# A four-layer graph network on one core: adding DMAs for the last mixture of experts, and GATv2 products and weight loads moved

## The chip, the cores and the metric

The kernel runs on one core of a Trainium2 chip, as one launch. The metric is the device time of that core in microseconds (us), the median of the runs. Engines are TensorE (PE in the profile, PEld for its weight loads), VectorE (DVE), ScalarE (ACT), GpSimd (POOL) and SyncE (SP). SP, ACT and POOL also issue DMAs; POOL issues the indirect ones, which gather or scatter rows by an index.

## What is computed

The input is a graph of 1250 nodes with 512 features, 20,000 edges and a loop at each node. Four layers follow one another. Each adds three things to the features `x`: a graph convolution and an attention over all nodes, both of the normed features, and then a feed-forward part (FFN).

- Layer 0: GATv2, itself three layers (per edge `leaky_relu(xl[src] + xr[dst] + ef)`, a logit, a softmax over each target's edges, a weighted sum of `xl[src]`); linear attention; eight experts with Sinkhorn routing.
- Layer 1: GAT, two layers; full attention over all nodes; eight experts of which two are taken.
- Layer 2: EGConv; linear attention; ten experts of which two are taken.
- Layer 3: GCN; linear attention; 32 experts with a capacity, of which two are taken.

The last FFN of the reference, which the change rewrites, is this (two experts a node, K = 2, and C = 98 rows an expert):

```python
C = int(np.ceil(CAPACITY_FACTOR * BTK / N))
probs = jax.nn.softmax(x_flat @ Wg, axis=-1)
vals, idx = jax.lax.top_k(probs, K)
...
keep = pos < C
dest = jnp.where(keep, a * C + pos, N * C)
buf = jnp.zeros((N * C, D), x.dtype).at[dest].set(x_flat[token], mode='drop')
h = jax.nn.relu(jnp.einsum('ncd,ndh->nch', buf, W1) + b1[:, None, :])
o = (jnp.einsum('nch,nhd->ncd', h, W2) + b2[:, None, :]).reshape(N * C, D)
gathered = o[jnp.minimum(dest, N * C - 1)]
y_flat = jax.ops.segment_sum(gathered * w[:, None], token, num_segments=BT)
y_flat = jnp.where(contrib[:, None] <= 1e-12, x_flat, y_flat)
```

## The kernel before

Nodes lie on the partitions in ten tiles of 128 (`NT`); the last one has 98 nodes. Most products are fp32 on PE, 128 rows by 512 columns in four steps over the features. The framework orders each engine's instructions and puts in the waits; where the code says `manual_schedule(engines={Pool})`, POOL's instructions keep the order in which they are written. Each engine runs its own queue in order, its DMA issues among them. SBUF and PSUM buffers rotate in pools, so that a load into a buffer waits for the last reader of what it held.

*GATv2* (`gat_layer`, one call for each of three layers). Edges come in groups of four tiles of 128, four groups for a block of 103 targets. For a group, POOL gathers the source rows `xl` from a table in DRAM (`load`, through `gather`, L231), SP loads an index row `nb` and edge fields into `oh` (`fields`, L1257 and L1259), ACT makes a one-hot matrix of them (`onehot`, L1273), PE spreads the target rows over the edges with it (`right`, L1286, L1287, and L1289, which adds `xl` on PE in every second of the first 20 steps), DVE forms the logits (L1299, L1302), and PE sums up by target (L1353). `load` runs three groups ahead of the edge steps and `fields` two. When a block of targets is done, a short list of steps (`finish`) norms it, transposes it (`across`, L1409) and, as soon as a whole tile of 128 nodes is there, makes the next layer's two tables for it (`gat_tables`): four products with `wl` and a store into `tl` (L1184), and four with `wr` and a store into `tr` (L1189), L1166 being the product. They pass through the queue `late` and take one PSUM bank, named `tab`. At the end of a layer a loop empties the queues; tiles 7, 8 and 9 come only there or shortly before. Gathers of the next layer read any row of `tl`, and so wait for its last store. From step 6 on, `prepare` loads the next layer's weights and vectors and works out its small vectors, a piece every third step.

*Layer 0's FFN* (`layer0_ffn`). Eight experts, each product's rows stored into `obuf` from ACT. Then 20 gathers on POOL bring back two rows for each node, DVE adds them by the gates (`add_scaled`, L1811), norms a tile, and PE transposes it (L160). Layer 1's attention (`global_attention`) loads four weights of 1 MB through `weight` (L141), and SP issues these as soon as a buffer is free. In the same stretch a counting of edges by pairs (L711) runs on PE between other steps, fed by loads on SP.

*Layer 2's FFN to layer 3* (`layer3_attn`). The experts' rows are stored into `routed_out` (L2367); `tail_steps` gives a function `need(t)`, which brings tile t of `xn` up through gathers (L231), adds (L2887), a norm and an affine step (L2896, L2897), a norm for the next layer and a transpose (L2386). SP loads four weights of 1 MB at the start (L141): the GCN's and three of the linear attention, of which ACT scales the last by 0.125 (L762).

*Layer 3's FFN* (`layer3_ffn`). 64 weight matrices of 1 MB stream in on SP (L3051), eleven ahead. Routing is worked out for all nodes at once on DVE. POOL scatters the normed rows into `routed_in` (20 DMAs, L239), at the row expert × 98 + place. Beside that, PE and DVE add the gated second biases, and the rows themselves for a node without an expert, into `x` (L3153, L185, L1811). For each expert ACT loads 98 rows `xe` (L3160), PE transposes them (L3164), DVE copies (L136), PE makes two products (L179 with ACT's relu, L3169; then L3173), the result is copied (L134 on ACT or L136 on DVE in turn) and stored into `routed_out` from ACT. After all 32, 20 gathers bring each node's two rows, `add_scaled` adds them by their gates, and SP stores each tile of `x` to the output.

Of the kernel before, what the change touches and what calls it, by code (L numbers as in the profile page):

```python
# [23 lines left out]
N = 1250  # L24
# [33 lines left out]
class Net:  # L58
# [79 lines left out]
    def weight(self, src, k, n):  # L138

        w = self.wp.tile([128, k, n], F32, tag="w", name="w")  # L140
        self.nc.sync.dma_start(w, src.rearrange("(k p) n -> p k n", p=128))  # L141
        return w
# [591 lines left out]
    def linear_attention_steps(self, xn, xT, w_qkv, w_out, b_out, qscale, finish, added=None,  # L734
                               need=None):
# [14 lines left out]
        with self.tc.tile_pool(name="la", bufs=1) as p, \  # L750
                self.tc.tile_pool(name="latmp", bufs=2) as tmp:
            wk = self.weight(w_qkv[:, D:2 * D], 4, D)
            wv = self.weight(w_qkv[:, 2 * D:3 * D], 4, D)
# [4 lines left out]
            for half in range(2):  # L758
                if half:
                    wq = self.weight(w_qkv[:, 0:D], 4, D)  # L760
                    if qscale != 1.0:
                        nc.scalar.mul(wq, wq, qscale)  # L762
# [446 lines left out]
    def gat_layer(self, L, p, xtab, otab, big):  # L1209
# [27 lines left out]
        step = [0]  # L1237

# [16 lines left out]
        def fields(g):  # L1255
            nb = p.tile([128, GE * 128], BF16, tag="nb", name="nb", bufs=4)
            nc.sync.dma_start(nb, self.nbt[g])  # L1257
            s = p.tile([128, GE * 128], F32R, tag="oh", name="oh", bufs=3)
# [102 lines left out]
        def finish(b):  # L1361
# [44 lines left out]
            def across():  # L1406
# [10 lines left out]
                for t in whole:  # L1417
                    for f in self.gat_tables(nxt, p, t, lambda c, t=t: X[t][:, c, :],
                                             lambda: self.bank("tab", [128, D])):
                        late.append((step[0] + 1, f))  # L1420
# [37 lines left out]
        fields(1)  # L1458
        onehot(0)
        prepared = prepare()  # L1460
        for i in range(FT + 3):
# [9 lines left out]
            if j == 2 and g + 2 < FG:  # L1471
                fields(g + 2)
            if i >= 6 and i % 3 == 0:
# [20 lines left out]
        bias_cur(NB - 1)  # L1494
        while edge or todo or late:
# [6 lines left out]
            for _ in range(2):  # L1502
                if late:
                    late.popleft()[1]()
        return nxt
# [24 lines left out]
    def layer0_ffn_to_layer1_attn(self):  # L1530
# [11 lines left out]
        with self.tc.tile_pool(name="l1a", bufs=1) as p:  # L1542
            xnT = p.tile([128, 4, NP], F32, name="xnT")
            with self.tc.tile_pool(name="l1b", bufs=1) as pb:
                xn = pb.tile([128, NT, D], F32, name="xn")
                with self.weights(), self.psum(3, 2, 3) if fast else self.psum():
                    count_pool()
                    self.counting = self.count_blocks(range(CB), True) if fast else iter(())
                    self.layer0_ffn(xn, xnT)
# [7 lines left out]
                    self.global_attention(xn, xnT, steps)  # L1557
# [91 lines left out]
    def layer0_ffn(self, xn, xnT):  # L1649
# [6 lines left out]
        with self.tc.tile_pool(name="l0f", bufs=1) as p, \  # L1656
# [126 lines left out]
            for t in range(NT):  # L1783
                for j in range(2):
                    g = tmp.tile([128, D], F32, tag="g", name="g", bufs=6)
                    self.gather(g, obuf[:, :], getI[:, t, j:j + 1])
                    self.add_scaled(t, g, G[:, t, j:j + 1])
                self.ready(t)
                self.norm_tile(t, xn[:, t, :])
                self.transpose_tile(xnT[:, :, t * 128:(t + 1) * 128], xn[:, t, :])  # L1790
                self.count(1)
            g1.close()

# [12 lines left out]

# [1451 lines left out]
```

## Time and profile before

| | |
|---|---|
| runs, us | 4461.85, 4464.39, 4471.24; median 4464.39 |
| profiled execution, us | 4489.82, span 4487.9 |
| mean granted clock of TensorE | 0.937 |
| last GATv2 product of a layer and the next layer's first (first boundary) | 750.93 and 765.70 |
| the same, second boundary | 1184.7 and 1189.32 |
| layer 0's FFN: first gather of `obuf`, PE idle before its next step | 1815.83, 16.24 |
| layer 2's FFN: first gather of `routed_out`, PE idle before its next step | 3736.03, 27.85 |
| layer 3's FFN: last scatter landed, first L179 product | 4200.62, 4204.76 |
| layer 3's FFN: last product ends, span ends | 4443.46, 4487.9 |

All times are microseconds from the start of the profiled span, or durations. In the page, a group is a line of the kernel, engine, operation, output and inputs, with its busy time and mean duration, and behind the last bar the time for which its engine stood idle before it and what ended that. In a table of windows each row gives a stretch, the busy time of each engine in it with the number of instructions, TensorE's granted clock, the share of the DMA engines' time and the rate. In a timeline a row gives start, duration, engine, line, operation and names, and in brackets the idle time before. In the chain of waits a row gives start, duration, and the work or wait that held up the end.

### The profile page before, as it was taken

How to read it: one execution, taken by the hardware profiler on the slowest of the kernel's cores; microseconds unless marked ns; L12 is line 12 of the kernel's file. 1: busy time of each engine (PE TensorE's matmuls, PEld its weight loads, DVE VectorE, ACT ScalarE, POOL GpSimd, SP SyncE). 2: the span in 40 equal slices, each digit the busy share in tenths (PEclk: the TensorE clock that was granted, in tenths of full speed). 3: DMA queues.
4: the chain of work that ended last, by engine and by line, in shares of the span. 5: the costliest groups of instructions: out<-in, count | busy, mean ns of one | idle time of the engine just before them, and what ended most of it. 6: DMA issues, size and time to landing. Idle time of an engine off the chain costs nothing. (4 is left out here: it accounts for less than half of the span.)

```text
span 4487.9 us, 49486 instructions
## 1 busy us (share of the span) xinstructions
PE 3922.2 (87%) x15466; PEld 2415.7 (54%) x15466; DVE 2689.5 (60%) x6338; ACT 1622.8 (36%) x2976; POOL 1351.0 (30%) x1308
## 2 busy tenths in 40 slices
PE   5987998899788867799999999997979896898796
PEld 3434554455354434444788877563546562455474
DVE  5357895888398865523896767314584225687301
ACT  2222442344133375110464446223451232554121
POOL 2017773776466501102000000103131013675102
PEclk9988999999899988899999999999989998997798
DMA  6437664666466423402421110383002653666695
GB/s 220 159 84 211 198 199 150 198 197 193 141 179 189 145 74 108 119 17 64 146 70 42 46 35 29 143 298 128 12 27 83 233 189 119 182 200 199 225 339 181
DMA packets 283001, 647.58 MB, mean 144 GB/s; under 512 B 61673, under 2 KB 108905, under 8 KB 267322
## 3 DMA queue, kind: packets, MB, share of 16 engines
q1 hardware_dynamic: 169290, 357.13, 24.1%
q0 software_dynamic: 73088, 234.75, 18.3%
q10 hardware_dynamic: 40352, 52.44, 3.4%
q8 instruction: 127, 2.08, 0.2%
q14 instruction: 144, 1.18, 0.1%
HBM read 528.87 MB, written 120.65 MB: 145 GB/s over the span
## 5 line engine op out<-in xcount | busy, mean ns | idle before, releaser
L231 POOL DMA_INDIRECT xl<-xl,srcI x564 | 616.8, 1094 | 290.2 <-issue 137.8
L1353 PE MATMUL more<-xl,wT 128*128 128x512 f32 x1128 | 579.7, 601 | 14.5 <-ACT wT L1343 14.0
L1286 PE MATMUL mm<-hl,oh 121*128 121x512 f32 x564 | 419.1, 743 | 73.8 <-DVE s L1299 37.8
L1302 DVE SCALAR_TENSOR_TENSOR junk<-s,att 128x512 f32<-128x512 f32 x534 | 417.9, 783 | 6.8
L1299 DVE TENSOR_TENSOR s<-xl,mm 128x512 f32<-128x512 f32 x534 | 357.8, 679 | 104.0 <-PE mm L1287 48.4
L2129 PE MATMUL more<-hh,e 128*128 128x259 f32 x1600 | 383.7, 385 | 11.7 <-ACT o L2072 8.6
L2129 PEld LDWEIGHTS more<-hh,e 128*128 128x128 f32 x1600 | 295.1, 191 | 75.8 <-issue 17.8
L171 PE MATMUL mm<-w,xnT 128*128 128x512 f32 x640 | 307.8, 620 | 16.6 <-ACT xnT L2388 12.1
L231 POOL DMA_INDIRECT hs<-gcn_h,srcI x188 | 214.6, 1142 | 93.6 <-issue 30.8
L1353 PEld LDWEIGHTS more<-xl,wT 128*128 128x128 f32 x1128 | 196.1, 192 | 74.8 <-issue 27.9
L1287 PE MATMUL mm<-hl,oh 121*128 121x512 f32 x564 | 236.4, 419 | 0.0
L1286 PEld LDWEIGHTS mm<-hl,oh 121*128 121x128 f32 x564 | 111.0, 197 | 215.5 <-issue 117.1
L231 POOL DMA_INDIRECT g<-routed_out,getI x60 | 67.6, 1126 | 488.5 <-DMA routed_out<-o 416.4
L2049 ACT ACTIVATE e<-r,hh 128x512 f32<-128x512 f32 (+1 forms) x240 | 154.2, 646 | 130.7 <-PE more L2129 119.5
L171 PEld LDWEIGHTS mm<-w,xnT 128*128 128x128 f32 x640 | 123.4, 198 | 144.0 <-issue 124.6
L3011 PE MATMUL more<-hl,oh 128*128 128x512 f32 x376 | 161.5, 534 | 30.9 <-DVE oh L2975 10.9
L1273 ACT ACTIVATE oh<-nb 112x512 fp32r<-112x512 bf16 x141 | 88.7, 630 | 273.6 <-DMA nb<-nbt 162.3
L2052 ACT ACTIVATE e<-r,a 128x512 f32<-128x512 f32 (+1 forms) x240 | 152.3, 646 | 71.1 <-DVE e L2054 57.8
L711 PE MATMUL more<-ohs,ohb 128*128 128x512 bf16 x564 | 137.5, 383 | 42.8 <-ACT ohs L695 18.0
L2054 DVE TENSOR_TENSOR e<-e,e 128x512 f32<-128x512 f32 (+1 forms) x240 | 141.5, 596 | 51.2 <-ACT e L2049 44.8
L1287 PEld LDWEIGHTS mm<-hl,oh 121*128 121x128 f32 x564 | 112.4, 199 | 110.1 <-issue 108.4
L1166 PE MATMUL tab<-w,xT 128*128 128x512 f32 x320 | 163.5, 605 | 9.0 <-ACT xT L1415 6.1
(631 smaller groups left out, 7787.8 us busy)
## 6 DMA issues: line engine op xcount, KB each, us to landing
w<-L_ffn_Wp SPq DMA_DIRECT2D x64, 1024.0 KB
w<-L_ffn_table SPq DMA_DIRECT2D x56, 1025.0 KB
neg<-ntab SPq DMA_DIRECT2D x80, 320.0 KB
nb<-nbt SPq DMA_DIRECT2D x141, 128.0 KB
hl<-xr SPq DMA_DIRECT2D x36, 448.0 KB
xr<-tro SPq DMA_DIRECT2D x30, 512.0 KB
xe<-routed_in SPq DMA_DIRECT2D x56, 256.0 KB
routed_out<-o ACTq DMA_DIRECT2D x56, 256.0 KB
```

Source lines behind the costliest of these rows:

```text
L171: self.nc.tensor.matmul(p, lhsT=xT[:, c, t * 128:(t + 1) * 128], rhs=w[:, c, n0:n0 + n], start=c == 0, stop=c == k - 1)
L231: self.nc.gpsimd.indirect_dma_start(out=out, out_offset=None, in_=table, in_offset=bass.IndirectOffsetOnAxis(ap=idx, axis=0), bounds_check ...
L1166: nc.tensor.matmul(d[name], lhsT=xT(c), rhs=L[name][:, c, :], start=c == 0, stop=c == 3)
L1286: nc.tensor.matmul(m, lhsT=s, rhs=hl[:K, 0, :], start=True, stop=False)
L1287: nc.tensor.matmul(m, lhsT=s, rhs=hl[:K, 1, :], start=False, stop=not on_pe(i))
L1299: nc.vector.tensor_tensor(o, d["xl"][:, j, :D], s, op=ALU.add)
L1302: nc.vector.scalar_tensor_tensor(junk, s, 0.0, L["att"], op0=ALU.max, op1=ALU.mult, accum_out=d["lg"][:, j:j + 1])
L1353: nc.tensor.matmul(B[b]["y"], lhsT=d["wT"][:, j, :], rhs=d["xl"][:, j, :D], start=k == 0 and j == 0, stop=last and j == GE - 1)
L2049: nc.scalar.activation(e1[:, :n], R[q, k, 0][:, :n], AF.Exp, bias=HH[q][:, s, 256:257])
L2052: nc.scalar.activation(e2[:, :n], R[q, k, 1][:, :n], AF.Exp, bias=heads[q][0][:, s, 0:1])
L2129: nc.tensor.matmul(ys[j], lhsT=e[:, j * 128:(j + 1) * 128], rhs=HH[q][:, s, :], start=s == 0, stop=s == NT - 1)
L3011: nc.tensor.matmul(y, lhsT=oh, rhs=hl[:, i], start=i + j == 0 and not (self.fast and k), stop=last and i + j == GE)
```

## The change

Five things change; the rest stays.

- *Layer 3's FFN.* The normed rows are two words wider (`xn` is 514 wide): the first of the two holds the node's number, which `iota` writes. They are scattered into a table of their own, `rin3`, which `clear_places` has filled beforehand with zeros and with row numbers beyond the nodes (1280 and up). A second table, `gtab`, holds for each node its first expert's number and its two gates. After the biases each tile of `x` is stored to the output on ACT. The node numbers of all places are loaded at once, in four DMAs on ACT (`tok`), ahead of the loads of `xe`. For each expert POOL gathers the gates of its rows from `gtab` (`fetch`), five experts ahead; DVE picks the one that belongs to this expert (`d`, three operations on 98 × 1), multiplies the result by it on its way out of PSUM, and POOL adds the 98 rows into the output by an indirect DMA with `compute_op=ALU.add`. The 32 stores, 20 gathers, 20 adds and ten output stores at the end are gone. The output has 1408 rows rather than 1250: rows 1280 and up take the unused places, and the host keeps the first 1250.
- *GATv2 products by target.* Of tiles 7, 8 and 9 the four `wr` products and the store into `tr` are held back and issued by the next layer, after its first `fields`, `load` and `onehot` and before its first step. In the ending loop the table products take `mm` banks rather than the `tab` bank.
- *GATv2 fields.* `fields` runs three groups ahead rather than two, with a fifth buffer for `nb` and a fourth for `oh`; `prepare` begins at step 15 rather than 6.
- *Layer 0's FFN to layer 1.* Of the attention's weights only `wk` is loaded ahead of the gathers; `wv` is loaded behind a POOL `memset` that stands after the last gather in POOL's fixed order. `clear_places` issues 34 stores on SP at the start of layer 1's attention.
- *Layer 2's FFN to layer 3.* The three weights of the linear attention are loaded behind three POOL `memset`s that come after `need(0)`; the GCN's weight stays where it was.

The core of the diff:

```diff
-    def weight(self, src, k, n):
+    def weight(self, src, k, n, behind=False):
 
         w = self.wp.tile([128, k, n], F32, tag="w", name="w")
+        if behind:
+            self.nc.gpsimd.memset(w[:1, 0, :1], 0.0)
...
-            nb = p.tile([128, GE * 128], BF16, tag="nb", name="nb", bufs=4)
+            nb = p.tile([128, GE * 128], BF16, tag="nb", name="nb", bufs=5)
...
-            s = p.tile([128, GE * 128], F32R, tag="oh", name="oh", bufs=3)
+            s = p.tile([128, GE * 128], F32R, tag="oh", name="oh", bufs=4)
...
-                    for f in self.gat_tables(nxt, p, t, lambda c, t=t: X[t][:, c, :],
-                                             lambda: self.bank("tab", [128, D])):
+                    fs = self.gat_tables(nxt, p, t, lambda c, t=t: X[t][:, c, :],
+                                         lambda: self.mm() if ending[0] else
+                                         self.bank("tab", [128, D]))
+                    if t >= NT - 3:
+                        rest.extend(fs[5:])
+                        fs = fs[:5]
+                    for f in fs:
...
+        fields(2)
         onehot(0)
+        for f in L.pop("rest", ()):
+            f()
         prepared = prepare()
...
-            if j == 2 and g + 2 < FG:
-                fields(g + 2)
-            if i >= 6 and i % 3 == 0:
+            if j == 2 and g + 3 < FG:
+                fields(g + 3)
+            if i >= 15 and i % 3 == 0:
...
+        ending[0] = True
...
+        if nxt is not None:
+            nxt["rest"] = rest
...
+            wk = self.weight(I["L1_mix_WkT"], 4, D)
+            with self.tc.manual_schedule(engines={mybir.EngineType.Pool}):
+                for t in range(NT):
+                    for j in range(2):
+                        g = tmp.tile([128, D], F32, tag="g", name="g", bufs=6)
+                        self.gather(g, obuf[:, :], getI[:, t, j:j + 1])
+                        self.add_scaled(t, g, G[:, t, j:j + 1])
+                    self.ready(t)
+                    self.norm_tile(t, xn[:, t, :])
+                    self.transpose_tile(xnT[:, :, t * 128:(t + 1) * 128], xn[:, t, :])
+                    self.count(1)
+                wv = self.weight(I["L1_mix_WvT"], 4, D, behind=True)
...
+    def clear_places(self, p):
+
+
+        nc = self.nc
+        self.rin3 = self.dram.tile([32 * CAP, D + 2], F32, name="routed_in3")
+        self.gtab = self.dram.tile([NP + 128, 4], F32, name="gates3")
+        zero = p.tile([128, D + 2], F32, name="zero3")
+        nc.gpsimd.memset(zero, 0.0)
+        nc.sync.dma_start(self.gtab[NP:, :], zero[:, :4])
+        nc.sync.dma_start(self.out[NP:, :], zero[:, :D])
+        nc.gpsimd.iota(zero[:, D:D + 1].bitcast(I32), pattern=[[0, 1]], base=NP,
+                       channel_multiplier=1)
+        for e in range(32):
+            nc.sync.dma_start(self.rin3[e * CAP:(e + 1) * CAP, :], zero[:CAP])
...
+            wk, wv = ws
+            self.clear_places(p1)
...
+                if t == 0 and behind is not None:
+                    behind()
...
+            def load():
+                ws.extend(self.weight(I["L3_mix_w_qkvT"][:, i:i + D], 4, D, behind=True)
+                          for i in (D, 2 * D, 0))
+
+            need = self.tail_steps(xn, xnT, load)
...
-            xn = p.tile([128, NT, D], F32, name="xn")
+            xn = p.tile([128, NT, D + 2], F32, name="xn")
+            nc.gpsimd.memset(xn[:, :, D:], 0.0)
+            nc.gpsimd.iota(xn[:, :, D].bitcast(I32), pattern=[[128, NT]], base=0,
+                           channel_multiplier=1)
...
-                        self.scatter(self.rin, putI[:r, t, j:j + 1], xn[:r, t, :], "moe")
+                        self.scatter(self.rin3, putI[:r, t, j:j + 1], xn[:r, t, :], "moe")
+
+                nc.vector.tensor_tensor(
+                    prod, ohs[0], self.iota[:, :NE].unsqueeze(1).to_broadcast([128, NT, NE]),
+                    op=ALU.mult)
+                nc.vector.memset(gate, 0.0)
+                nc.vector.tensor_reduce(gate[:, :, 0], prod, AX.X, ALU.add)
...
+                nc.vector.tensor_copy(gate[:, :, 1:3], w0)
+                nc.sync.dma_start(self.gtab[:NP, :].rearrange("(t p) c -> p t c", p=128), gate)
...
+                r = rows(t)
+                nc.scalar.dma_start(self.out[t * 128:t * 128 + r, :], self.x[:r, t, :])
+
+            tok = p.tile([CAP, NE], I32, name="tok")
+            for i in range(0, NE, 8):
+                nc.scalar.dma_start(
+                    tok[:, i:i + 8].bitcast(F32),
+                    self.rin3[i * CAP:(i + 8) * CAP, D].rearrange("(e c) -> c e", c=CAP))
+            gates = {}
+
+            def fetch(e):
+                gates[e] = tmp.tile([CAP, 4], F32, tag="g", name="g", bufs=8)
+                self.gather(gates[e], self.gtab[:, :], tok[:, e:e + 1])
+
+            for e in range(5):
+                fetch(e)
             for e in range(NE):
                 w1, w2 = ws[2 * e], ws[2 * e + 1]
                 er = slice(e * CAP, (e + 1) * CAP)
-                xe = tmp.tile([CAP, D], F32, tag="xe", name="xe", bufs=3)
-                nc.scalar.dma_start(xe, self.rin[er, :])
+                xe = tmp.tile([CAP, D], F32, tag="xe", name="xe", bufs=4)
+                nc.scalar.dma_start(xe, self.rin3[er, :D])
+                if e + 5 < NE:
+                    fetch(e + 5)
+
+                g = gates.pop(e)
+                d = tmp.tile([CAP, 2], F32, tag="d", name="d", bufs=4)
+                nc.vector.tensor_scalar(d[:, :1], g[:, :1], float(e), None, op0=ALU.is_equal)
+                nc.vector.tensor_tensor(d[:, 1:], g[:, 1:2], g[:, 2:3], op=ALU.subtract)
+                nc.vector.scalar_tensor_tensor(d[:, 1:], d[:, :1], d[:, 1:], g[:, 2:3],
+                                               op0=ALU.mult, op1=ALU.add)
...
-                o = tmp.tile([CAP, D], F32, tag="o", name="o")
-                self.evac(o, y)
-                nc.scalar.dma_start(self.rout[er, :], o)
+                o = tmp.tile([CAP, D], F32, tag="o", name="o", bufs=3)
+                nc.vector.tensor_scalar(o, y, d[:, 1:], None, op0=ALU.mult)
+                nc.gpsimd.indirect_dma_start(
+                    out=self.out, out_offset=bass.IndirectOffsetOnAxis(ap=tok[:, e:e + 1],
+                                                                         axis=0),
+                    in_=o, in_offset=None, bounds_check=NP + 127, oob_is_err=True,
+                    compute_op=ALU.add)
...
-            for t in range(NT):
-                for j in range(2):
-                    g = tmp.tile([128, D], F32, tag="g", name="g", bufs=4)
-                    self.gather(g, self.rout[:, :], getI[:, t, j:j + 1])
-                    self.add_scaled(t, g, w0[:, t, j:j + 1])
-                r = rows(t)
-                nc.sync.dma_start(self.out[t * 128:t * 128 + r, :], self.x[:r, t, :])
...
-    out = nc.dram_tensor("out", (N, D), F32, kind="ExternalOutput").ap()
+    out = nc.dram_tensor("out", (NP + 128, D), F32, kind="ExternalOutput").ap()
```

## The prediction

> **What bounds the kernel now.** I read the page first, then the windows of the places that the change touches, the chain of waits at the end, and the timelines there. The page gives the frame.
>
> ```profile
> span 4487.9 us, 49486 instructions
> PE 3922.2 (87%) x15466; PEld 2415.7 (54%) x15466; DVE 2689.5 (60%) x6338; ACT 1622.8 (36%) x2976; POOL 1351.0 (30%) x1308
> PE   5987998899788867799999999997979896898796
> L231 POOL DMA_INDIRECT g<-routed_out,getI x60 | 67.6, 1126 | 488.5 <-DMA routed_out<-o 416.4
> ```
>
> TensorE (PE) is busy 87% of the span, so a gain is either PE work that comes into an idle stretch, or an idle stretch made shorter. The slices below nine are where stages meet. The last row is the gathers that close three of the four FFNs: they wait for the last expert's store. The windows (PE, PE weight load, DVE, ACT, POOL, clock, DMA share, GB/s) show what is idle where.
>
> ```profile
> 760.00:800.00 40.00, 24.12 (x64) 12.85 (x65) 20.53 (x52) 1.89 (x3) 32.17 (x34) 0.76 0.79 237
> 1800.00:1840.00 40.00, 15.28 (x94) 12.34 (x92) 20.23 (x45) 5.10 (x15) 18.89 (x19) 0.67 0.84 219
> 3720.00:3760.00 40.00, 10.78 (x35) 5.25 (x34) 18.01 (x43) 7.83 (x14) 16.07 (x14) 0.65 0.55 180
> 4220.00:4240.00 20.00, 20.00 (x129) 14.84 (x128) 1.60 (x3) 5.54 (x14) 0.00 (x0) 1.00 0.95 332
> 4460.00:4488.00 28.00, 0.00 (x0) 0.00 (x0) 10.52 (x14) 0.00 (x0) 13.36 (x12) 0.50 0.63 198
> ```
>
> A GATv2 layer's start (760) leaves PE 15.9 of 40 us idle; the two gather stages (1800, 3720) leave 24.7 and 29.2 idle. In the last FFN's experts PE is never idle, beside DMA at 95%. After 4460 PE does nothing at all. The chain of waits shows that tail:
>
> ```profile
> 4439.99 3.45 PE mm L3173 x8
> 4443.46 0.59 ACT o L134
> 4444.07 2.95 DMA routed_out<-o
> 4456.27 4.64 DMA g<-routed_out,getI
> 4468.67 4.90 DMA g<-routed_out,getI
> 4476.85 5.24 DMA g<-routed_out,getI
> 4482.19 0.75 DVE x L1811
> ```
>
> From the last product's end (4443.46) to the span's end there are 44.4 us, of one store, 20 gathers and their adds. The start of the same stage, in the timeline:
>
> ```profile
> 4197.98 0.99 POOL L239 DMA_INDIRECT routed_in<-xn,putI  x1 [0.30 <-issue]
> 4200.64 4.46 ACTq L3160 DMA_DIRECT2D xe<-routed_in  x5
> 4203.18 1.27 PEld L3164 LDWEIGHTS tp<-ident,xe 98*128 98x128 f32 x8 [6.54 <-DMA xe<-routed_in]
> 4204.76 6.15 PE L179 MATMUL mm<-xT,w 128*128 128x98 f32 x32
> ```
>
> The last scatter is issued at 4197.98, the first expert's rows are asked for at 4200.64, once it has landed, and the first product runs at 4204.76. And a GATv2 boundary, on PE:
>
> ```profile
> 747.23 3.70 PE L1166 MATMUL tab<-w,xT 128*128 128x512 f32 x8 [0.69 <-ACT xT L1415]
> 752.34 3.70 PE L1166 MATMUL tab<-w,xT 128*128 128x512 f32 x8 [1.41 <-DVE junk L1182]
> 765.70 0.79 PE L1286 MATMUL mm<-hl,oh 121*128 121x512 f32 x1 [9.66 <-DVE s L1299]
> ```
>
> Table products are 3.70 us a tile and side (four fp32 products; the trace counts two matmuls for each). The next layer's first product stands 14.8 us after the last left product (750.93 to 765.70), and only one right product lies in there.
>
> **What the Trainium skill says.** "DMA: Bandwidth & Descriptors", section "SWDGE vs HWDGE vs iDMA": adding during a DMA can be issued from GpSimd alone, so the adds into `out` stand on POOL's queue. No DMA of the trace of before adds. Section "Rules for kernel authors": an adding DMA reads its destination and writes it later, and the next one on the same bytes must wait for its semaphore. In the order of instructions of the changed kernel each add does wait for the one before. Section "Latency and other measured facts": HBM access grows from 0.2 us on average to 2 us at high load. The trace agrees in direction: the 196 KB `routed_out` store lands in 2.95 us at the quiet end, and in 5.1 to 6.6 us in the saturated stretch. Section "Issuing engines are not separate DMA queues": transfers from all engines interleave on the same 16. The trace agrees: an `obuf` store of layer 0 lands in 5.3 us behind four 1 MB weight loads, a `routed_out` store of layer 2 in 6.1 us behind four, and in 2.0 us without.
>
> **The change part by part.** The sum is made against the profiled execution: 4489.8 us, 4487.9 of it span. The runs' median, 4464.4, is 25.4 lower, and I take the difference over unchanged.
>
> *Last FFN, end.* Removed: 32 stores, 20 gathers, 20 adds, the output's stores at the end: 44.4 us after the last product. Added there: the gated copy on DVE (0.6, by the 0.59 copy of before), and one adding scatter. A plain scatter of 128 rows lands 2.64 us after its issue (4197.98 to 4200.62). The adding one reads first: 0 to 1.5 us more (no run shows it; the upper end is what a loaded gather takes over an unloaded scatter, 4.0 against 2.6). I take 4.4 after the copy: end 5.0, so −39.4.
>
> *Last FFN, start.* Between the last scatter's landing and the first product there now stand a load of token numbers (784 pieces of four bytes), gate gathers 0 to 3, and DVE's `d` of experts 0 to 3, which the order of instructions puts ahead of the copy of `xT` for expert 0. Token load: 2.5 us, by the first `xe` (4200.64 to 4203.14). Four gathers at POOL's pitch of 1.3 us (the pitch of the scatters at 4195.39, 4196.67, 4197.98): 3.9 to the fourth's issue, and 2.6 to its landing. Then `d` and `xT`, 1.0. First product at 4200.6 + 10.0 = 4210.6, where it was 4204.76: +6. On ACT the token loads and output stores also go ahead of `xe`(0), some eight issues at 0.33; that is inside the same wait. Ends: 0 if the copy gets past, +12 if the small pieces take 6 us more. Weights don't get late by it: they run ahead.
>
> *Last FFN, in the loop.* An expert takes PE 6.95 us (32 from 4204.76 to 4443.46, some overlap at the ends, PE 20.00 of 20). Each adding scatter waits for the landing of the one before, so the period is the larger of 6.95 and a landing L. L is the unknown: 2.6 unloaded, plus the 2.2 to 3.7 that the saturated stretch adds to a store, plus 0 to 1.5 for the read: 4.8 to 7.8. I take 6.8, no bound, plus 4 us for single late ones (`o` has three buffers, 20 us of cover). At 7.8 it is 32 × 0.85 = 27 us. DMA bytes rise by one read of 0.2 MB per expert, 0.6 us at 340 GB/s and 17 us over 27 experts; the last weight lands at 4410.8 and is used about 4440, so 29 us of slack hold it. Gate fetch (POOL, idle), `d` (three tiny DVE operations; DVE has 1.6 of 20 us) and the POOL `iota` and `memset` cost nothing on the path. Extra DVE at the routing (product, reduce, copy, some 1.2 us) lies beside 20 scatters at 1.3.
>
> Together: −39.4 + 6 + 4 = −29.
>
> *GATv2, two boundaries.* Right products of tiles 7, 8 and 9 go from the ending of a layer to ahead of the next layer's first product. Tiles 7 and 8, 7.4 us, leave a stretch where PE works (31.5 of 40 us in 720 to 760); three times 3.7 = 11.1 us then fit in the 14.8 us hole. The gain is at most 7.4 per boundary; I take 6, because the drain has gaps of its own: −12. The right side's stores (SP) and copies (DVE) move with them; the first block's rows don't need them, and the weight load still stands just ahead of the left store, so the hole stays. If the hole were filled (gathers earlier), the products would cost their 11 us again.
>
> *GATv2, fields one group earlier, preparation later.* At a layer's start POOL is busy 32.2 of 40 us, so gathers feed it, but PE waits also for one-hots behind `nb` (ACT waits 11.9 us for it once in 756 to 830) and for logits. Of about 10 us idle after the first product I take 3 in each of three layers: −9. Ends: 0 (POOL is the bound) and −24.
>
> *Layer 0's FFN to layer 1.* One weight load, not four, goes before the gathers: the store's landing falls from 5.3 to some 3, and 20 gathers run on a freer DMA: −4. Against it, 34 stores of zeros go on SP ahead of the counting's loads: 34 × 0.35 = 12 us of issue and 6.5 MB, 30 us at 219 GB/s. PE uses those loads from about 1861, 18 us after the last gather: +2. Net −2; ends −8 and +8.
>
> *Layer 2's FFN to layer 3.* Three of four loads go behind the twelfth gather (POOL memset, then SP): the last store lands in 3 to 4 rather than 6.1 us: −3. ACT's scaling of the query weight now waits for 3 MB, some 15 us from 3755, and the copies of `xnT` are queued behind it, with PE waiting for them: ends −4 and +4.
>
> Sum: −29 − 12 − 9 − 2 − 3 = −55. So 4489.8 − 55 = 4434.8 profiled, and 4464.4 − 55 = 4409.4 in the runs; I say 4410.
>
> **The rivals.**
> 1. *GATv2 gives nothing*: the start of a layer is bound by gathers, so what leaves the drain comes back there. For: POOL 32.2 of 40. Against: the PE hole of 9.66 us holds moved products whatever POOL does. −55 + 21 = −34: 4430.
> 2. *Everything cover-limited comes free*: copies pass `d`, the landing stays under 6.9, GATv2 gains 35: −39.4 + 2 − 35 − 5 = −77: 4387. For: 16 us of PE idle at each layer start.
> 3. *The chain of adds becomes the bound*, slower than before. It decides from L = 6.95 + (39.4 − 6 + 26)/32 = 8.8 us. For: DMA at 95 to 99% in the stretch, and 2 KB reads and writes queued behind 1 MB loads. Against: 8.8 is above my upper end of 7.8, and a slower period itself empties the queues. At L = 10: 32 × 3.05 = 98, less 59: +39: 4503.
> 4. *The same chain, in part*: L = 7.8 to 8.5, +27 to +50 for my 4: −32 to −9: 4432 to 4455, I name 4445.
>
> **How the numbers follow.** Forecast 0.46 (4392 to 4428 for its own range), rival 1 0.19, rival 2 0.14, rival 4 0.12, rival 3 0.09. The range takes in rivals 1 and 4 and most of 2: 4380 to 4455. Faster or slower counts beyond 0.2%, 8.9 us, about what a measurement of this kernel can tell from no change. Faster: forecast, 1, 2 and most of 4, 0.87; same: the end of 4, 0.04; slower: rival 3, 0.09.
>
> **What would show it.** After the last expert's product some 5 us, not 44. First L179 of that stage 10 us after the last scatter's landing. Period of L179 6.95 us there, and adding scatters that land in under it; if they land in 8 or more, with POOL waiting for `out` and PE for DVE's `o`, rival 3 or 4. At the GATv2 boundaries three right products between the last left one and the first L1286-like product; if the hole grows with them, rival 1. I am wrong in sign if the adds take 9 us each.

## The result, and the profile after

The changed kernel takes 4439.26 us (median; 4435.64 to 4446.19), the kernel before 4464.39 in the same series: a ratio of 0.9949, 95% interval 0.9937 to 0.9961, so 25 us or half a per cent faster. The forecast was 54 us. The direction and the range hold; the size is less than half of what was forecast.

The profiled execution after lies 7 us above its median, the one of before 25. Their difference, 4487.9 − 4444.4 = 43.5 us of span, is therefore no measure of the change; the stages below say where the excess of before sat.

The page of the changed kernel, its frame:

```profile
span 4444.4 us, 49688 instructions
PE 3920.1 (88%) x15466; PEld 2412.3 (54%) x15466; DVE 2700.2 (61%) x6432; ACT 1611.9 (36%) x2960; POOL 1409.4 (32%) x1360
PE   5987998899888867798999999997979896998698
```

The windows after, for the stages shown for before (the first three are placed 10, 30 and 20 us earlier, because the stages come earlier):

```profile
750.00:790.00 40.00, 30.48 (x99) 16.58 (x98) 28.07 (x77) 8.95 (x17) 31.80 (x35) 0.91 0.84 261
1770.00:1810.00 40.00, 14.90 (x80) 10.99 (x79) 21.24 (x49) 5.09 (x15) 21.17 (x20) 0.67 0.68 171
3700.00:3740.00 40.00, 12.00 (x28) 5.27 (x28) 24.93 (x66) 8.36 (x19) 26.18 (x26) 0.65 0.57 191
4220.00:4240.00 20.00, 19.96 (x119) 14.10 (x119) 3.21 (x13) 4.60 (x13) 6.24 (x6) 1.00 0.99 345
4300.00:4320.00 20.00, 18.10 (x102) 12.36 (x101) 3.06 (x12) 3.63 (x11) 4.56 (x5) 0.91 0.92 290
4430.00:4444.00 14.00, 0.84 (x2) 0.00 (x0) 0.75 (x1) 0.00 (x0) 2.24 (x2) 0.70 0.23 33
```

In the experts PE was busy 20.00 of 20 before; by 4300 it now has gaps (18.10). POOL at a GATv2 start is as busy as it was (31.80 of 40). The two gather stages have as little PE work as before.

The end of the chain of waits, after:

```profile
4418.73 4.44 DMA out<-o,tok
4423.17 0.02 issue
4423.19 0.02 POOLq L3257
4423.21 0.53 issue
4423.74 0.03 POOLq L3257
4423.77 0.22 issue
4423.98 4.41 DMA out<-o,tok
...
4429.22 4.69 DMA out<-o,tok
...
4434.73 1.51 POOL out L3257
```

The gathers are gone from the end, but not replaced by one scatter: the chain is a row of adding scatters, each issued 0.8 us after the one before has landed. PE's last product ended at 4430.85, with one scatter on its way and one still to be issued. The start of the same stage, in the timeline:

```profile
4156.71 0.97 POOL L241 DMA_INDIRECT routed_in<-xn,putI  x1 [0.30 <-issue]
4162.26 1.08 POOL L233 DMA_INDIRECT g<-gates,tok  x1 [4.58 <-DMA tok<-routed_in]
4163.99 0.42 ACTq L3231 DMA_DIRECT2D xe<-routed_in  x1
4166.71 0.92 PE L3244 MATMUL tp<-ident,xe 98*128 98x98 f32 x4 [3.51 <-DMA xe<-routed_in]
4171.06 0.22 DVE L3239 SCALAR_TENSOR_TENSOR d<-d,g 98x1 f32<-98x1 f32 x1
4171.19 0.56 DVE L136 COPY xT<-tp 128x392 f32<-128x392 f32 x1
4171.81 5.93 PE L181 MATMUL mm<-xT,w 128*128 128x98 f32 x32 [4.18 <-DVE xT L136]
```

The last scatter landed at 4159.37. The first rows are asked for at 4163.99, 4.6 us later, because token loads and output stores stand ahead of them on ACT; in the kernel before they were asked for at once. Their transpose is done at 4167.6, and its copy waits until 4171.19 behind `d` of expert 3. And the first GATv2 boundary on PE, one line of before and then after:

```profile
766.29 1.91 PE L1289 MATMUL mm<-xl,ident 128*128 128x512 f32 x2
```

```profile
733.30 16.84 PE L1172 MATMUL mm<-w,xT 128*128 128x512 f32 x32 [0.59 <-ACT xT L1423]
756.91 2.07 PE L1297 MATMUL mm<-xl,ident 128*128 128x512 f32 x2 [5.84 <-DMA xl<-xl,srcI]
```

The 32 matmuls are four times eight: the last left product and three right ones stand together now. The last lines are where PE adds the first gathered rows of the next layer, and that is the place to compare: the product at 765.70, which the table of before calls the next layer's first, is its fourth, since three of the layer's 188 `right` products ran there at 741.54 already, ahead of the last table products. After, PE waits 5.84 us for the gathered rows.

The stages of all kernels, from one profiled execution each (us, by PE's products: from the first `right` of the first GATv2 layer to the last sum by target of the third; from the last expert's products of layer 2's FFN to the last sum by target of layer 3's GCN; from there, over the routing, to the first expert product; first to last expert product; from there to the span's end):

```
kernel         GATv2   L3 attention  routing  experts  end
before         1254.9     401.2        79.9    238.7   44.5
only_l0        1237.5     389.1        80.0    239.5   43.7
only_l2        1234.4     387.4        80.1    238.6   44.3
only_l3        1232.9     393.0        88.4    259.9   12.9
only_gat       1223.0     398.5        80.0    239.1   44.8
gat_rest       1230.1     397.6        80.1    238.1   44.2
gat_fields     1238.1     396.0        80.1    238.7   44.5
after          1226.2     388.4        88.3    259.0   13.6
plain_scatter  1219.2     382.7        88.0    242.8   13.7
half_weights   1222.8     389.6        88.2    242.6   11.1
after_again    1217.5     388.5        88.1    258.4   13.8
start          1224.3     391.1        81.4    262.2   11.0
two_tables     1223.9     388.5        88.1    241.7   17.3
two_start      1223.9     386.7        81.4    239.5   18.8
```

Three other kernels with GATv2 as before (only_l0, only_l2, only_l3) take 1233 to 1238 us for it where the profiled execution of before took 1255, and the five with layer 3's attention as before take 3 to 12 us less there. That is its excess over the median; it has nothing to do with the change, and why it was slow there isn't shown. In the last three columns before agrees with the kernels that keep these stages to within 1 us.

### The profile page after: what moved, and what is told of

The parts are those of the page before. It is cut to its first block, busy times and chain, and to the rows that moved or that the text cites. A ratio compares the mean times of both kernels' runs of the same rounds, so it can differ in the third digit from the quotient of the medians.

```text
span 4444.4 us, 49688 instructions
## 1 busy us (share of the span) xinstructions
PE 3920.1 (88%) x15466; PEld 2412.3 (54%) x15466; DVE 2700.2 (61%) x6432; ACT 1611.9 (36%) x2960; POOL 1409.4 (32%) x1360
## 5 line engine op out<-in xcount | busy, mean ns | idle before, releaser
L1294 PE MATMUL mm<-hl,oh 121*128 121x512 f32 x564 | 416.6, 739 | 32.6 <-DVE s L1307 16.1
L1295 PE MATMUL mm<-hl,oh 121*128 121x512 f32 x564 | 229.6, 407 | 0.0
L2030 PE MATMUL mm<-w,xnT 128*128 128x258 f32 x640 | 159.0, 392 | 5.2 <-DVE junk L2014 4.7
L3017 ACT ACTIVATE hl<-hs,rec 128x512 fp32r<-128x512 f32 x188 | 130.6, 717 | 90.4 <-PE more L3057 42.3
```

Source lines behind the costliest of these rows:

```text
L1294: nc.tensor.matmul(m, lhsT=s, rhs=hl[:K, 0, :], start=True, stop=False)
L1295: nc.tensor.matmul(m, lhsT=s, rhs=hl[:K, 1, :], start=False, stop=not on_pe(i))
L2030: nc.tensor.matmul(m, lhsT=chunk(layer, c)[:, t * 128:(t + 1) * 128], rhs=w[:, c, :], start=c == 0, stop=c == k - 1)
```

## The experiments

All ratios are to the kernel before, measured alongside, with their 95% intervals; gains in us are worked out from the ratios where nothing else is said.

**The parts alone.** Four kernels, each the kernel before with one part of the diff. First the last FFN (with `clear_places`):

> The kernel before with the last FFN's part of the change alone, the 34 stores of zeros included. Theory: the tail's gain is eaten up by a start that is 8 us later and a loop that is 20 us longer, because each adding scatter waits for the one before and these land in some 8 us beside the weight loads: 4464 - 2 = about 4462, between 4455 and 4470. Rival (forecast: the loop stays at PE's pace, and what is missing of the gain is elsewhere): 4464 - 29 = about 4435.

Measured: 4465.41 us, ratio 0.9985 (0.9977 to 0.9994), 7 us (3 to 10). The theory holds: routing +8.5, experts +21.2, end −31.6 in the table, together −2. GATv2's part:

> The kernel before with the GATv2 part of the change alone: right products of tiles 7 to 9 held back for the next layer, fields three groups ahead, preparation from step 15. Theory (the stage marks of the two traces hold): the end of GATv2 comes some 28 us earlier, 4464 - 28 = about 4436. Rival (the profiled execution of before was slow in this stage, since it lies 25 us above its median, and the gain there is mostly that): 4464 - 8 = about 4456, and the stage in this kernel's own trace stands within 10 us of an equal stage in the other kernels that keep the old GATv2.

Measured: 4457.14 us, ratio 0.9973 (0.9962 to 0.9983), 12 us (8 to 17). The trace's 28 us are out: more than half of them were the excess of the profiled execution before. The rival's 8 us stand at the edge of the interval, and the stage in this kernel's own trace is 10 to 15 us shorter than in the three kernels with the old one, so the gain is rather more than the rival said. The two loads' parts:

> The kernel before with the moved weight loads of layer 1's attention alone (one load ahead of the gathers, the others behind), without the 34 stores of zeros. Theory: the store before the gathers lands earlier, but the last FFN product to the first transpose stays at 16 us, as the traces of before and after show (16.2 and 16.9): gain 0 to 3 us, about 4463. Rival (forecast): 4 us or more, 4460 or less.

Measured: 4469.99 us, ratio 1.000 (0.999 to 1.001): nothing, give or take 4 us. The earlier landing is there: the last store lands 2.3 us after its issue, 5.3 in before. But from the first gather to the first transpose 13.3 us pass rather than 11.3, so a good part of it is lost again on the way (one execution each).

> The kernel before with the moved weight loads of layer 3's linear attention alone. Theory: about 4 us from the earlier landing of the last store before the gathers, and some 8 us from a better order later in the stage, as the marks of the two traces show (12.6 us in all): 4452. Rival (forecast): 3 us, 4461.

Measured: 4467.24 us, ratio 0.9988 (0.9981 to 0.9995): 5 us (2 to 8): near the forecast's 3, and the theory's 12 are out. Here the last store lands in 2.0 rather than 6.1 us, and the way from the first gather to the first transpose stays at 20.0 us, so the gain is kept. The four ratios add up to 0.9946 (−0.27, 0.00, −0.12 and −0.15 per cent, 24 us); the whole has 0.9949. So no interaction of the parts shows.

**GATv2 in two halves.** One with the held-back products (`rest`, `ending`, and the call after `onehot(0)`), one with the fields and the preparation:

```diff
-            if j == 2 and g + 2 < FG:
-                fields(g + 2)
-            if i >= 6 and i % 3 == 0:
+            if j == 2 and g + 3 < FG:
+                fields(g + 3)
+            if i >= 15 and i % 3 == 0:
```

> The kernel before with only the held-back right products of GATv2 (and the free banks for the ending); fields and preparation as before. Theory (the whole gain of the GATv2 part is the drain, 5 to 6 us at the end of each of the first two layers, and the products' new place is free because the hole waits for gathers anyway): the same 0.27% as the whole part, 12 us. Rival (the two halves share it): 0.13% or less.

Measured: 4464.23 us, ratio 0.9982 (0.9974 to 0.9990), 8 us (4 to 12). That lies between the two figures; the theory's 0.27% is just outside the interval, the rival's 0.13% inside.

> The kernel before with only the earlier fields and the later preparation of GATv2. Theory (the start of a layer goes at the pace of the gathers, 1.3 us and more a tile on POOL, and neither fields nor preparation change that): no change, within 0.1%. Rival (forecast: some 3 us for each of three starts): 9 us, 0.2% faster.

Measured: 4472.34 us, ratio 1.0006 (0.9996 to 1.0015). The rival's 0.2% is out: the fields alone give nothing; the held-back products give most of the gain, not surely all. Whether the fields help once the products are out of the way (0.9973 together, 0.9988 by multiplying the halves) is inside the intervals and stays open.

The traces show the gain at both boundaries. From the last `right` product of a layer to the first add of gathered rows in the next it took 64.1 to 66.9 us at the first boundary in the five kernels with the old order, and takes 58.8 to 62.5 in the nine with the new one; at the second, 62.3 to 63.7 and 55.7 to 56.6. That is some 5 and 7 us. The second layer's own stretch in between is alike in both groups, about 355 to 362 us, so nothing of it is seen to come back there.

**Why the adds are late.** Two kernels take one suspect each away from the changed kernel. In the first the scatter no longer adds:

```diff
-                    in_=o, in_offset=None, bounds_check=NP + 127, oob_is_err=True,
-                    compute_op=ALU.add)
+                    in_=o, in_offset=None, bounds_check=NP + 127, oob_is_err=True)
```

> The changed kernel with the addition left out of the last FFN's scatters (plain writes, same rows, same waits), so the rows are only overwritten. Theory (the landing is long because of the queueing behind the weight loads, and the read of the addition adds a share of it): with the quiet landing falling from 4.4 to about 2.7 us and the loaded one from 7.7 to about 6, the loop comes down from 259 to about 240 us, and the run ends some 20 us earlier than the changed kernel. Rival (the write behind the loads alone is what takes long): the loaded landing stays at 7 us or more and the loop at 250 or more.

Measured: 4423.52 us, ratio 0.9904 (0.9882 to 0.9927), against 0.9949 and 0.9952 for the changed kernel: 20 us, as the theory said. In the second, half of the weights stay away:

```diff
-                w1, w2 = ws[2 * e], ws[2 * e + 1]
+                w1, w2 = ws[e // 2 * 2], ws[e // 2 * 2 + 1]
...
-                for i in range(2):
-                    if ahead < 2 * NE:
+                for i in range(2 * (e % 2)):
+                    if ahead < NE:
```

> The changed kernel with half of the last FFN's weight loads left out (two experts use the same two matrices), adding scatters as they are. Theory (saturation by the loads makes the landings long): with DMA at half load an adding scatter lands in 4.5 to 5.5 us, under PE's 6.95, and the loop comes down from 259 to about 240 us. Rival (the addition is slow whatever else runs, or the chain's own turnaround is the bound): the period of the scatters stays above 7.5 us and the loop above 250.

Measured: 4426.69 us, ratio 0.9904 (0.9882 to 0.9927), again the theory's size. Either alone brings the loop back to 243 us. Landings in us from the start of POOL's instruction to the last semaphore update, means of scatters 2 to 24; pitch is the distance of two issues:

```
kernel         mean landing   shortest, longest   mean pitch of the first 24   last six, mean
after              8.09          4.50, 11.72              8.97                     4.47
plain_scatter      6.55          4.30,  8.02              7.56                     3.29
half_weights       4.81          4.43,  6.37              7.49                     4.53
```

The first of the plain kernel's last six, 4.29, was issued while the last weight was landing; the other five take 2.96 to 3.33.

PE alone needs 7.46 us an expert in the kernel before (238.7 over 32) and 7.58 in `half_weights` (242.6 over 32), where no scatter holds it up. In the changed kernel a landing of 8.09 and a turnaround of 0.88 on POOL make 8.97, well over that. With half the weights they make 4.81 + 0.88 = 5.69, well under it, and the pitch is PE's. With plain writes they make 6.55 + 0.88 = 7.43, about PE's own pace: most of these scatters still go out as soon as the one before has landed, but the buffers absorb it. POOL in the timeline, of the changed kernel and of the one with half the weights:

```profile
4290.53 1.52 POOL L3257 DMA_INDIRECT out<-o,tok  x1 [2.47 <-DMA out<-o,tok]
4292.36 1.07 POOL L233 DMA_INDIRECT g<-gates,tok  x1 [0.30 <-DVE o L3256]
4299.26 1.52 POOL L3257 DMA_INDIRECT out<-o,tok  x1 [5.83 <-DMA out<-o,tok]
...
4311.85 1.52 POOL L3257 DMA_INDIRECT out<-o,tok  x1 [9.69 <-DVE o L3256]
```

```profile
4275.96 1.52 POOL L3257 DMA_INDIRECT out<-o,tok  x1 [4.08 <-DVE o L3256]
4277.79 1.07 POOL L233 DMA_INDIRECT g<-gates,tok  x1 [0.30 <-issue]
4283.93 1.52 POOL L3257 DMA_INDIRECT out<-o,tok  x1 [5.06 <-DVE d L3238]
4290.91 1.53 POOL L3257 DMA_INDIRECT out<-o,tok  x1 [4.08 <-DVE o L3256]
```

The gather of gates goes out at once, and then POOL stands until the scatter has landed, in the last line too, where the profile names `o`: the scatter of 4299.26 took 11.72 us and landed at 4310.98. With half the weights it waits for `o` or, by the profile, for `d`, long done: in both cases for PE's product. The waits of the gated copy (and of PE for it) in the experts' loop, in us in total, times and longest; changed kernel and then half weights:

```profile
DVE o L3256 <- PE mm L3253: 111.8, 18, 9.5
DVE o L3256 <- DMA out<-o,tok: 91.3, 12, 10.4
PE mm L181 <- DVE o L3256: 11.3, 8, 2.5
```

```profile
DVE o L3256 <- PE mm L3253: 199.8, 32, 10.3
```

Twelve of the copies wait for a scatter to free one of the three `o` buffers, none with half the weights or with plain writes. PE in turn waits for the copy, which holds its PSUM bank. So it goes from the scatter back to `o`, from `o` to PSUM, and to PE.

**Mending it.** Three kernels from the changed one, and that one again beside them.

> The changed kernel itself, for the comparison in the same call: 0.995 of the kernel before, and an adding scatter every 9 us while the weights stream.

Measured: 4448.32 us, ratio 0.9952 (0.9935 to 0.9968), a scatter every 8.95 us.

```diff
+            rows_of(0)
+            rows_of(1)
             tok = p.tile([CAP, NE], I32, name="tok")
...
-                g = gates.pop(e)
-                d = tmp.tile([CAP, 2], F32, tag="d", name="d", bufs=4)
...
                 o = tmp.tile([CAP, D], F32, tag="o", name="o", bufs=3)
```

Here `rows_of` is the load of `xe`, two experts ahead, and the lines of `d` stand just ahead of `o`.

> The changed kernel with the last FFN's start in another order: the first two loads of expert rows go ahead of the token numbers, and the gate of an expert is worked out ahead of its gated copy rather than ahead of the copy of its transposed rows. Theory (the start is late because those rows and that copy stand behind token numbers and gate gathers): from the last scatter's landing to the first product some 4 us rather than 12.5, and the run ends 6 to 8 us earlier than the changed kernel. Rival (the chain of adds decides the end whatever the start does, since its pace is set by the weight stream): within 2 us of the changed kernel.

Measured: 4440.02 us, ratio 0.9925 (0.9906 to 0.9943); 8 us by the medians, though the interval overlaps that of the changed kernel: the theory's 6 to 8 us fit, but the rival isn't excluded. Against `after_again` the routing part fell by 6.7 us and the loop grew by 3.8: some of the early start is waited for again in the chain. In the timeline the first product now follows the last scatter's landing (4158.70) by 5.6 us, where the changed kernel has 12.4:

```profile
4158.73 0.34 ACTq L3218 DMA_DIRECT2D xe<-routed_in  x1
4162.38 0.57 DVE L136 COPY xT<-tp 128x392 f32<-128x392 f32 x1 [4.51 <-PE tp L3247]
4164.27 2.03 PE L181 MATMUL mm<-xT,w 128*128 128x98 f32 x8
```

Then the second table:

```diff
-                    out=self.out, out_offset=bass.IndirectOffsetOnAxis(ap=tok[:, e:e + 1],
+                    out=self.odd[:, :] if e % 2 and e < 26 else self.out,
+                    out_offset=bass.IndirectOffsetOnAxis(ap=tok[:, e:e + 1],
...
+                if e == 26:
+                    for t in range(NT):
+                        r = rows(t)
+                        nc.gpsimd.dma_start(out=self.out[t * 128:t * 128 + r, :],
+                                            in_=self.odd[t * 128:t * 128 + r, :],
+                                            accum_op=ALU.add, max_dma_last_dim=4 * D)
```

`odd` is filled with zeros in `clear_places`, by eleven more stores.

> The changed kernel with the adding scatters of experts 0 to 26 alternating between the output and a second table, which is added to the output by ten plain adding DMAs behind expert 26. Theory (the serial landing of the adds is the bound, not the adds themselves): each scatter has two periods to land, the loop goes at PE's pace (238 to 243 us rather than 259), and the run ends 14 to 20 us earlier than the changed kernel, about 0.991 of the kernel before. Rival (two adds in flight slow each other and the loads, or the merge holds up the last five experts by more than they have to spare): less than 6 us earlier.

Measured: 4434.55 us, ratio 0.9922 (0.9907 to 0.9936); 14 us by the medians, with intervals that just touch. The loop is at 241.7 us, although the adds land more slowly than before (9.2 us on average for scatters 2 to 24): additions, weight loads and the gated copy on DVE are all still there, and only the wait for the add just before is gone. That is the most direct sign that the serial landing was the bound. Both together:

> Both of the edits above together. If they are independent: 20 to 28 us earlier than the changed kernel, about 0.989 of the kernel before. If the start is only hidden time: no more than the two tables alone.

Measured: 4424.34 us, ratio 0.9902 (0.9883 to 0.9921): 24 us by the medians below `after_again`, with intervals apart, as if the two edits were independent (8 and 14). This version beats both kernels. In its timeline the scatters come at PE's pace, in turn to the two tables, and the merge follows:

```profile
4279.38 1.54 POOL L3269 DMA_INDIRECT out<-o,tok  x1 [5.66 <-DVE d L3264]
4286.36 1.54 POOL L3269 DMA_INDIRECT odd<-o,tok  x1 [4.06 <-DVE d L3264]
4293.34 1.54 POOL L3269 DMA_INDIRECT out<-o,tok  x1 [4.08 <-DVE d L3264]
...
4372.73 8.53 POOL L3278 DMA_DIRECT2D out<-odd  x10 [3.30 <-DMA out<-o,tok]
4390.20 1.58 POOL L3269 DMA_INDIRECT out<-o,tok  x1 [8.94 <-issue]
```

From 4372.73 to 4390.20 the merge holds up the chain, and the last five scatters follow at 5.4 us, so the last lands 13 us after PE's last product. A later or smaller merge wasn't tried.

## Why the prediction was wrong

It was right in direction and wrong in size, and in one bound: it held that PE would go on setting the pace of the last loop, where the chain of adds came to set it. By parts, forecast and measured alone: last FFN −29 and −7; GATv2 −21 and −12; layer 0 to 1 −2 and 0; layer 2 to 3 −3 and −5. The shares of the last FFN below come from one execution each.

- **Last FFN, in the loop: the step that failed**, a mis-sized term. The prediction put the landing L of an add at 6.8 us, "no bound", and the loop at +4. L measured 8.09, just above the upper end of 7.8 that it gave, and the loop costs +20.3. Four things were in it:
  - Both parts of L came out at the top. A plain scatter under load takes 6.55, where 2.6 and the delay under load made 4.8 to 6.3. The addition takes 1.54 more (8.09 against 6.55), where 0 to 1.5 was allowed; 0.5 of it is POOL's longer instruction (1.52 against 1.00).
  - The delay under load was misread. In the trace of before the stores of the saturated stretch take 5.1 to 8.0 us, 6.1 on average, not 5.1 to 6.6. In quiet, behind the last weight, four of them take 2.26 to 2.35; the 2.95 is the very last one alone. So the load adds 3.8 on average, where the prediction had 3.7 as its extreme.
  - The pitch is not L but L + 0.88, the turnaround on POOL, which the sum left out.
  - PE's period was put at 6.95, where the prediction's own numbers give 238.7 / 32 = 7.46. That mistake went the other way.

  Rival 4, "the same chain, in part", has the mechanism, though the price was below its 27 to 50. The rule of the Trainium skill that the next adding DMA has to wait for the semaphore of the one before ("DMA: Bandwidth & Descriptors", "Rules for kernel authors") was cited, and the trace shows that wait; what it costs was not on record. Of the +20.3, 16 go when the adds or half of the loads are taken away. What the other 4 are isn't shown.
- **Last FFN, start.** +6 forecast, +8.3 measured. The copy's wait behind `d`, the mechanism named, is 3.6 of it; the other 4.6 are the late load of the first rows on ACT, which the prediction had taken to lie inside the same wait. The experiment that takes 6.7 back moves both at once.
- **Last FFN, end.** 5.0 us forecast, 13.6 measured: the chain's backlog is 3 us (previous scatter landed at 4433.91, PE done at 4430.85), the last scatter lands 5.2 later, and then 5.3 us pass until the span's end. In the kernel before 2.5 pass there; the prediction's 5.0 ended with the landing and had nothing for this.
- **GATv2, two boundaries.** −12 forecast; the held-back products alone gave 8 (4 to 12 by the interval), and the traces some 5 and 7 at the two boundaries. Right, in mechanism and size, though the hole was misread: its end at 765.70 is not the layer's first product, and the second boundary's is 4.6 us (1184.7 to 1189.32) where 14.8 was taken for both. What moved is that a layer's ending is shorter, and the next layer's gathers start earlier with it: at the second boundary 50 to 51 us after the last `right` product rather than 56 to 57.
- **GATv2, fields.** −9 forecast, nothing measured alone. Rival 1's reason fits here: POOL is busy 32 of 40 us at a layer's start before and after, and PE waits there for gathered rows. No run made the gathers faster, so this isn't shown.
- **The two load moves.** Within the ends that were given, or nearly: −5 (−2 to −8) for layer 2 to 3, where −4 was the end. The store's earlier landing, the mechanism named, is there in both; PE's wait ahead of its first transpose falls from 27.85 to 23.60 for layer 2 to 3, and for layer 0 to 1 it stays (16.24 and 16.92).
- **Rival 3, the sign.** Its point of decision was a pitch of 8.8 us, and the first 24 scatters came at 8.97. The sign held all the same, for two reasons: PE's own period is 7.46 rather than 6.95, so that each scatter costs 1.5 us and not 2.0; and once the weights have all landed (4396) an add takes 4.5 us, so that the last scatters catch up, where the rival counted all 32. The prediction had neither: that the sign came out right is in part luck.

## What to carry to other kernels

A chain of DMAs that each wait for the last has a period of its own, landing plus turnaround, and that has to be compared with the loop's period under the loop's own DMA load, not with a landing from a quiet stretch. Two destinations in turn give each landing two periods, and here that took the chain off the path, though each add took longer; the merge held up the chain for 17 us. And when one profiled execution lies well above the median of its kernel, stage differences between two traces can mislead by as much; kernels that keep a stage unchanged show what it normally takes.

## What was unexpected of the hardware

- An adding scatter of 98 rows of 2 KB keeps POOL busy for 1.52 us where a plain one takes 1.00, and it lands in 4.5 us in quiet where the plain one takes 3.0 to 3.3. In the records of the last scatters each of the 98 rows is a packet of 2 KB by itself; of the plain ones, 84 rows go in pairs, as 42 packets of 4 KB.
- Beside weight loads, at 290 to 345 GB/s, single adding scatters took up to 11.7 us.
- With two adds in flight (`two_tables`) each landed in 9.2 us on average, with one in 8.1, beside the same weight loads.
- POOL's closing instruction, a drain, ran from 4437.22 to 4443.57 in the changed kernel, 4.5 us beyond the landing of the last scatter, and with plain scatters 8.4 us beyond it. In the kernel before it ended at 4486.02, beside the last store.
